# A layer-normalised gated feed-forward block: another form of the normalisation, another split of its first halves, and one late sum on another engine

## The chip, the core and the metric

The kernel runs on one core of a Trainium2 chip. The metric is device time in microseconds (us). Five engines work side by side, each through its own instructions in order: TensorE (PE; its weight loads are listed as PEld), VectorE (DVE), ScalarE (ACT), GpSimd (POOL) and SyncE (SP), which here only issues DMAs.

## What is computed

The input x has 2 x 1024 tokens of 512 features, in fp32. Cut to what matters:

```python
xn  = (x - mean(x)) / sqrt(var(x) + 1e-5)             # per token
s   = einsum('bsk,nk->bsn', xn, weight * block_mask)  # 512 -> 512
nx  = xn * rsqrt(mean(xn**2) + 1e-5) * ln_w
h   = silu(nx @ gate_w.T) * (nx @ up_w.T)             # 512 -> 1792
out = x + s * silu(h @ down_w.T)                      # 1792 -> 512
```

## The kernel before

**Tiles.** The 2048 tokens are four token tiles t of 512, and each of these is four row tiles i of 128 tokens. `xt[t, i]` is a row tile in SBUF: 128 tokens on the partitions, 512 features along the free axis. Token tiles 0 and 1 are normalised in this form and then turned on PE: `transpose` (L173) writes a 128x128 piece into a PSUM bank `pt`, one bank for each block c of 128 features, and `evacuate` (L179) copies the bank to SBUF on ACT. Token tiles 2 and 3 come from memory already transposed and are scaled by rows of factors later; the change leaves their form as it is.

**Products.** The matrix products are done in a seven-product scheme on two levels. An outer product q takes sums of quarters of the operands, and within it an `instance` (L398) does seven inner products m = 1 to 7, in the order 1, 5, 2, 6, 3, 7, 4, into the PSUM banks X, Y and Z. A product is a 128x128 weight against 128x512 moving data; the profile shows each as two records of a matmul. Seven groups g of gate and up weights and an eighth of the masked linear layer make 56 instances: first q = 1 and 2 of every group, then q = 6, 5, 7, 3, 4 of each group. After them seven down instances of 25 to 33 products (L649) and the output follow.

**Who makes the operands.** `inner_b` (L274) makes the sums of the moving data on DVE and POOL; the first of them reads the bank `pt_1_0`, so it needs all four pieces of that bank. `inner_a` (L377) makes the sums of the weights on POOL, `scale_a` (L329) multiplies weights by `ln_w` in two halves of 256 columns (on POOL for group 0, on ACT for the others), and `summed` (L503) adds two partial results of product 7 of each group, for its four quarters i, on the engines that a tuple names.

**The normalisation.** `stats` (L131) makes mean and variance of a row tile on DVE, `stats_act` (L138) does it on ACT for row tile 1 of token tile 0. `factors` (L145) makes, for the four row tiles at once, `scl` = 1/sqrt(var) (a square root on ACT, L161, then a reciprocal on DVE, L158), and `nb` = -mean x scl (on DVE, L159). `normalise` (L163) then writes x x scl + nb over half a row tile, 128x256: L167 on DVE or POOL, L169 on ACT. The eight halves are dealt out by the lists at L782 (token tile 0) and L795 (token tile 1).

**What sets the order.** No scheduler does. Every step is recorded by `at(position, function)`, all steps are sorted by position and emitted in that order (L968), and this is the order on each engine's queue. One position stands for one product of PE; `T` (L748) turns a time in us, counted to 14.0 at position 0, into a position. So a position is an order and not a time: an instruction runs when those before it on its engine and what it waits for are done. Loads go through SP in the order of their positions. One of them, the second group of weights at L763, waits for a small memset on POOL (L761), and the loads of token tiles 2 and 3 stand behind it.

**Warming.** While the first tiles are loaded, PE runs 18 products of the identity (`warm`, L773), as soon as POOL has made the identity (L114).

Of the kernel before, what the change touches and what calls it, by code (L numbers as in the profile page):

```python
# [8 lines left out]
F32 = mybir.dt.float32  # L9
I32 = mybir.dt.int32  # L10
AF = mybir.ActivationFunctionType
ALU = mybir.AluOpType
AX = mybir.AxisListType

P = 128
W = 512
BLK = 32
EPS = 1e-5
# [13 lines left out]
def tile_masked_linear_gated_ffn(  # L32
# [11 lines left out]
    nc = tc.nc  # L44
    NT, H = x.shape
    KC = H // P
    G = gu.shape[0]
    NTT = NT // W
    TT = W // P
# [10 lines left out]
    small = ctx.enter_context(tc.tile_pool(name="small", bufs=2))  # L60
# [8 lines left out]
    def at(pos, fn, *args):  # L69
        events.append((pos, len(events), fn, args))  # L70
# [23 lines left out]
    def bank(tag, name):  # L94
        return ps.tile([P, W], F32, tag=tag, name=name, bufs=PSB[tag])

    def add(eng, o, a, b, op=ALU.add):
        eng.tensor_tensor(o, a, b, op)  # L98

    dve, pool, act = nc.vector, nc.gpsimd, nc.scalar  # L100
# [3 lines left out]
    eps2 = const.tile([P, 1], F32, tag="eps2", name="eps2")  # L104
# [3 lines left out]
    blockones = const.tile([P, P], F32, tag="blockones", name="blockones")  # L108
    keep = const.tile([P, 4, 16], F32, tag="keep", name="keep")

    def constants():
        nc.gpsimd.memset(eps2, EPS * EPS)
        nc.vector.memset(zero, 0.0)
        make_identity(nc, ident)  # L114
        nc.scalar.activation(stat_0, eps2, AF.Sqrt)
        nc.vector.memset(blockones, 0.0)
        for b in range(P // BLK):
            nc.gpsimd.memset(blockones[b * BLK : (b + 1) * BLK, b * BLK : (b + 1) * BLK], 1.0)


    xt, raw, stat = {}, {}, {}
    agg = small.tile([P, NTT, TT, 2], F32, tag="agg", name="agg", bufs=1)
# [22 lines left out]
    def factors(t, i=0, n=TT):  # L145


        if t < 2:
            scl = small.tile([P, n], F32, tag="scl", name=f"scl_{t}_{i}", bufs=3)
            nb = small.tile([P, n], F32, tag="nb", name=f"nb_{t}_{i}", bufs=3)  # L150
        else:
            scl, nb = fac[:, t - 2, 0, :], fac[:, t - 2, 1, :]
        for k in range(n):
            stat[t, i + k] = (scl[:, k : k + 1], nb[:, k : k + 1])
        rows = slice(i, i + n)

        def last():
            nc.vector.reciprocal(scl, scl)  # L158
            nc.vector.scalar_tensor_tensor(nb, agg[:, t, rows, 0], -1.0, scl, ALU.mult, ALU.mult)  # L159

        return [lambda: nc.scalar.activation(scl, agg[:, t, rows, 1], AF.Sqrt, bias=eps2, scale=1.0 + EPS), last]  # L161

    def normalise(t, i, eng, cols=slice(0, W)):  # L163
        scl, nb = stat[t, i]
        v = xt[t, i][:, cols]
        if eng is not act:
            eng.tensor_scalar(v, v, scl, nb, ALU.mult, ALU.add)  # L167
            return
        nc.scalar.activation(v, v, AF.Identity, bias=nb, scale=scl)  # L169

# [292 lines left out]
    def group(g, where):  # L463
        def tiles(i):
            return lambda k: mem[:, i + k, :]

        acc, v5, c1 = tiles(F["acc"] + 4 * (g % 2)), tiles(F["v5"] + 4 * (g % 2)), tiles(F["c1"] if g % 2 else F["vc"])
        vc = tiles(F["tmp"] + 2 if g % 2 else F["vc"])
        h11 = tiles(F["a1"])
        gate = {}  # L470

        def silu(key, t):
            gate[key] = bank("V", f"gate_{g}_{key[2]}")
            nc.scalar.activation(gate[key], t(), AF.Silu)  # L474

        hs, hpos = {}, {}

        def h_out(key, a, b, n):
            nc.vector.tensor_mul(a(), gate[key], b())  # L479
            hs[key] = a()  # L480
            q = {(0, 0): 1, (1, 0): 2, (1, 1): 3}.get(key[:2])
            if q:
                nc.sync.dma_start(h_dram[HD[q], g, n], a())

        def done(R, Hh, tiles):

            ready = {}

            def after(i, pos):
                r, n = divmod(i, 2)  # L490
                if g == G:
                    at(pos + 1, lambda: nc.sync.dma_start(s_dram[2 * R + r, 2 * Hh + n], tiles(i)))
                    return
                ready[i] = pos
                if n in ready and n + 2 in ready:
                    key = (R, Hh, n)
                    p = max(ready[n] + 1.2, ready[n + 2] - 0.5, SILU)
                    at(p, silu, key, lambda: tiles(n))
                    hpos[key] = max(p, ready[n + 2]) + (3.9 if key == (1, 1, 0) else 1.3)
                    at(hpos[key], h_out, key, lambda: tiles(n), lambda: tiles(n + 2), n)  # L500
            return after

        def summed(dst, src, into, then=None, engines=(pool,) * 4):  # L503

            def after(i, pos):
                at(pos + 1.2, lambda: add(engines[i], into(i), dst(i), src(i)))
                if then:
                    then(i, pos + 3.2)
            return after

        nothing = lambda i, pos: None
        setup = {
            1: (None, acc, nothing),
            2: (acc, c1, done(0, 0, c1)),
            6: (acc, acc, nothing),
            5: (None, v5, summed(v5, acc, vc)),
            7: (acc, acc, summed(v5, acc, v5, done(1, 1, v5), (dve, dve, pool, pool) if g < G else (pool,) * 4)),
            3: (vc, vc, done(0, 1, vc)),
            4: (acc, acc, done(1, 0, acc)),
        }  # L520
        for q in setup:
            instance(where[g, q], g, q, *setup[q])

        def h_sum(q, n, tile_of, a, b):

            o = hs[q, n] = tile_of()
            add(pool, o, hs[a + (n,)], hs[b + (n,)], ALU.subtract)
            nc.sync.dma_start(h_dram[HD[q], g, n], o)

        sums, rest = slots(F["acc"] + 4 * (g % 2), 4), 7 * where[g, BLOCKS[0]]  # L530
        at(7 * where[g, 1] + 15, lambda: nc.sync.dma_start(acc_dram[g], sums))
        at(rest - (14 if g else 6), lambda: nc.sync.dma_start(sums, acc_dram[g]))
        if g < G:
            def again():
                nc.sync.dma_start(slots(F["a1"], 2), h_dram[HD[1], g].rearrange("n p w -> p n w"))
                hs.update({(0, 0, n): h11(n) for n in range(2)})
            at(rest + 24, again)
            pos = 0
            for n in (1, 0):
                for q, t, i, a, b in ((5, vc, n + 2, (0, 1), (0, 0)), (7, v5, n + 2, (1, 1), (0, 1)),  # L540
                                      (6, vc, n, (1, 1), (5,))):
                    pos = max(pos, hpos[0, 1, n], hpos[1, 1, n]) + 1.45
                    at(pos, h_sum, q, n, lambda t=t, i=i: t(i), a, b)
            for n in (1, 0):
                pos = max(pos, hpos[1, 0, n]) + 1.45
                at(pos, h_sum, 4, n, lambda n=n: acc(n + 2), (1, 0), (6,))
# [201 lines left out]
    T = lambda us: (us - 14.0) / 0.86  # L748
# [30 lines left out]
    at(T(4.2), stats_act, 0, 1)  # L779
    for t, p, step in ((1, T(11.9), 0), (3, 23.2, 0.6), (2, 36.1, 1.2)):  # L780
        plan(p, step, factors(t))
    for us, i, h, eng in ((7.45, 3, 0, dve), (7.46, 2, 0, dve), (7.45, 0, 0, act), (7.95, 1, 0, act), (8.45, 0, 1, act), (7.47, 1, 1, dve),  # L782
                          (8.5, 2, 1, pool), (8.6, 3, 1, pool)):
        at(T(us), normalise, 0, i, eng, slice(h * W // 2, (h + 1) * W // 2))
    for us, i, cs in ((7.96, 3, (0,)), (7.97, 0, (0,)), (7.98, 2, (0,)), (7.99, 1, (0,)), (8.70, 3, (1,)), (8.71, 0, (1,)), (8.72, 2, (1,)),
                      (8.73, 1, (1,)), (9.25, 0, (2, 3)), (9.26, 1, (2, 3)), (9.7, 2, (2, 3)), (9.71, 3, (2,)), (9.72, 3, (3,))):
        for c in cs:
            at(T(us) + 0.0001 * c, transpose, 0, c, i, "XYYX"[c])
    for i in range(TT):
# [2 lines left out]
        at(T(8.2 + 0.82 * i), stats, 1, i)  # L792
        for c in range(KC):
            at((T(14.35), T(14.8), T(15.25), 4.1)[c] + 0.06 * i, transpose, 1, c, (2, 0, 3, 1)[i], "XVVV"[c])
    for us, i, h, eng in ((12.3, 2, 0, dve), (12.4, 3, 0, dve), (12.5, 2, 1, dve), (12.4, 0, 0, act), (12.5, 1, 0, act),  # L795
                          (12.6, 0, 1, act), (12.6, 3, 1, pool), (12.7, 1, 1, pool)):
        at(T(us), normalise, 1, i, eng, slice(h * W // 2, (h + 1) * W // 2))
    at(T(6.0), scale_a, 0, 0, pool, (0,))
    at(T(8.7), scale_a, 0, 0, pool, (1,))
    at(T(10.3), scale_a, 0, 1, pool)  # L800
    for c in range(KC):
# [20 lines left out]
    for n, p0 in ((1, 31), (0, 50)):  # L822
        t = 2 + n
# [24 lines left out]
    for g in range(G + 1):  # L848
# [8 lines left out]
        if g:  # L857
            plan(p - 7, 1, inner_a(g, 1))
        else:
            for us, fn in zip((10.0, 10.0, 12.5, 12.5), inner_a(0, 1, 0, 1)):  # L860
                at(T(us), fn)
            plan(2.75, 0, inner_a(0, 1, 1, 1))
        ahead = 2 if g == G else 0
# [151 lines left out]
```

## Time and profile before

| what | value |
|---|---|
| three runs | 505.7, 506.1, 506.34 us; median 506.1 us |
| profiled execution | 506.55 us, of which the span of the instructions is 504.7 us |
| PE busy | 498.9 us, 99% |
| DVE / ACT / POOL busy | 379.6 (75%) / 187.6 (37%) / 356.4 (71%) us |
| granted TensorE clock | 1.00 |
| PE records | 784 of the products at L408, mean 593 ns, one started every 0.43 us where nothing holds them |
| DMA | 124.75 MB, 247 GB/s over the span |

The times of a profile count from the first instruction, so the span leaves out 506.55 - 504.7 = 1.85 us around it. PE's matmuls overlap, and a matmul that waits inside this pipeline hardly shows as idle time. So PE is not read by its busy share here but by the starts of its instructions: four 128x512 records in 1.72 us are the steady step, and whatever a piece of the chain takes above this is a wait. A line of the timeline is: start, length, engine, line, operation, output<-inputs, how many in a row; in brackets the engine's idle time before it and what ended it. A line of the chain of waits is: start, length, and what the chain spent it on.

### The profile page before, as it was taken

How to read it: one execution, taken by the hardware profiler on the slowest of the kernel's cores; microseconds unless marked ns; L12 is line 12 of the kernel's file. 1: busy time of each engine (PE TensorE's matmuls, PEld its weight loads, DVE VectorE, ACT ScalarE, POOL GpSimd, SP SyncE). 2: the span in 40 equal slices, each digit the busy share in tenths (PEclk: the TensorE clock that was granted, in tenths of full speed). 3: DMA queues.
4: the chain of work that ended last, by engine and by line, in shares of the span. 5: the costliest groups of instructions: out<-in, count | busy, mean ns of one | idle time of the engine just before them, and what ended most of it. 6: DMA issues, size and time to landing. Idle time of an engine off the chain costs nothing.

```text
span 504.7 us, 4924 instructions
## 1 busy us (share of the span) xinstructions
PE 498.9 (99%) x1223; PEld 226.7 (45%) x1223; DVE 379.6 (75%) x582; ACT 187.6 (37%) x363; POOL 356.4 (71%) x301
## 2 busy tenths in 40 slices
PE   8999999999999999999999999999999999999997
PEld 7444444444444444444444444444444444444444
DVE  6977887876968969697896989969647644377636
ACT  5666776634535363343535342330100101001111
POOL 4728997464896959879696988975672764649960
PEclk9999999999999999999999999999999999999999
DMA  6879847268168595866959594699996798467372
GB/s 213 295 234 339 293 169 249 113 251 304 62 232 308 187 309 194 303 237 234 307 188 311 190 317 161 227 352 369 359 336 230 239 394 309 133 247 265 108 229 86
DMA packets 62365, 124.75 MB, mean 247 GB/s; under 512 B 5984, under 2 KB 13824, under 8 KB 60288
## 3 DMA queue, kind: packets, MB, share of 16 engines
q1 hardware_dynamic: 62192, 124.43, 69.7%
q8 instruction: 10, 0.16, 0.1%
q14 instruction: 19, 0.16, 0.1%
q10 hardware_dynamic: 144, 0.00, 0.0%
HBM read 78.25 MB, written 46.15 MB: 247 GB/s over the span
## 4 chain that ended last, share of the span: by engine, by line
PE 97%; DVE 1%; DMA 1%; SPq 0%; issue 0%; ACT 0%; ACTq 0%
PE x L408 38%; PE y L408 19%; PE dx L656 15%; PE z L408 10%; PE dy L656 8%; PE dz L656 5%; PE dv L656 1%; PE pt L176 1%; DMA mem<-in_x 1%; PE part L667 1%; DVE st L133 0%; DVE mem L167 0%; SPq L129 0%; DVE agg L134 0%; ACT scl L161 0%
## 5 line engine op out<-in xcount | busy, mean ns | idle before, releaser
L98 POOL TENSOR_TENSOR mem<-mem 128x512 f32<-128x512 f32 (+4 forms) x261 | 322.4, 1258 | 111.5 <-ACT mem L436 30.5
L408 PE MATMUL x<-mem 128*128 128x512 f32 x448 | 211.6, 593 | 0.0
L408 PEld LDWEIGHTS x<-mem 128*128 128x128 f32 x448 | 84.4, 190 | 107.2 <-issue 89.9
L98 DVE TENSOR_TENSOR mem<-x,mem 128x512 f32<-128x512 f32 x137 | 93.4, 686 | 39.0 <-PE x L408 37.4
L408 PE MATMUL y<-mem 128*128 128x512 f32 x224 | 114.6, 593 | 0.1
L656 PE MATMUL dx<-mem 128*128 128x512 f32 x174 | 78.3, 592 | 0.0
L98 DVE TENSOR_TENSOR mem<-mem 128x1536 f32<-128x1536 f32 (+3 forms) x51 | 67.0, 1318 | 6.9 <-PE dx L656 4.4
L98 DVE TENSOR_TENSOR mem<-y,mem 128x512 f32<-128x512 f32 x96 | 65.9, 686 | 7.6 <-PE y L408 6.1
L415 ACT COPY z<-x 128x512 f32<-128x512 f32 x54 | 31.0, 573 | 94.7 <-PE x L408 90.7
L408 PEld LDWEIGHTS y<-mem 128*128 128x128 f32 x224 | 42.2, 190 | 53.1 <-issue 46.7
L408 PE MATMUL z<-mem 128*128 128x512 f32 x112 | 57.2, 593 | 0.0
L656 PEld LDWEIGHTS dx<-mem 128*128 128x128 f32 x174 | 33.1, 190 | 41.6 <-issue 41.1
L656 PE MATMUL dy<-mem 128*128 128x512 f32 x98 | 44.5, 592 | 0.0
L474 ACT ACTIVATE gate<-mem 128x512 f32<-128x512 f32 x56 | 32.7, 602 | 20.4 <-DVE mem L98 15.9
L479 DVE TENSOR_TENSOR mem<-gate,mem 128x512 f32<-128x512 f32 x56 | 38.2, 683 | 1.9 <-ACT gate L474 1.5
L629 POOL TENSOR_TENSOR mem<-mem 128x512 f32<-128x512 f32 x16 | 25.5, 1602 | 14.0 <-DMA mem<-s_dram 13.8
L639 ACT ACTIVATE silu<-mem 128x512 f32<-128x512 f32 (+1 forms) x16 | 9.2, 575 | 64.3 <-DVE mem L98 48.0
L408 PEld LDWEIGHTS z<-mem 128*128 128x128 f32 x112 | 21.1, 190 | 25.8 <-issue 21.9
L98 DVE TENSOR_TENSOR mem<-z,mem 128x512 f32<-128x512 f32 x41 | 28.1, 685 | 2.6 <-PE z L408 2.5
L656 PEld LDWEIGHTS dy<-mem 128*128 128x128 f32 x98 | 18.6, 190 | 23.4 <-issue 23.4
L98 DVE TENSOR_TENSOR mem<-dx,mem 128x512 f32<-128x512 f32 x16 | 11.1, 692 | 20.5 <-PE dx L656 20.4
L656 PE MATMUL dz<-mem 128*128 128x512 f32 x56 | 25.2, 592 | 0.0
(94 smaller groups left out, 287.6 us busy)
## 6 DMA issues: line engine op xcount, KB each, us to landing
h_dram<-mem SPq DMA_DIRECT2D x98, 256.0 KB, 2.4
mem<-h_dram SPq DMA_DIRECT2D x28, 768.0 KB, 6.3
mem<-in_gu SPq DMA_DIRECT2D x42, 256.0 KB, 4.1
acc_dram<-mem SPq DMA_DIRECT2D x8, 1024.0 KB, 4.0
mem<-acc_dram SPq DMA_DIRECT2D x8, 1024.0 KB, 6.2
mem<-in_x_t SPq DMA_DIRECT2D x24, 256.0 KB, 5.5
mem<-in_x SPq DMA_DIRECT2D x16, 256.0 KB, 4.6
s_dram<-mem SPq DMA_DIRECT2D x16, 256.0 KB, 5.6
```

Source lines behind the costliest of these rows:

```text
L98: eng.tensor_tensor(o, a, b, op)
L176: nc.tensor.transpose(pt[t, c][:, i * P : (i + 1) * P], xt[t, i][:, c * P : (c + 1) * P], ident)
L408: nc.tensor.matmul(st[key], weights(g, q, m), operand(q, m), start=first and not (key == "z" and seeded), stop=True, skip_group_check=True)
L415: nc.scalar.copy(st["z"], st["x"])
L474: nc.scalar.activation(gate[key], t(), AF.Silu)
L479: nc.vector.tensor_mul(a(), gate[key], b())
L629: at_later.append(lambda: nc.gpsimd.tensor_tensor(s_tile, s_tile, rms_bc[t], ALU.mult))
L639: nc.scalar.activation(b[0][:, part], y[:, part] if source is None else source(), AF.Silu)
L656: nc.tensor.matmul(st[key], w(), b(), start=first and key != "z", stop=True, skip_group_check=True)
L667: nc.tensor.matmul(st[part.start][:, part], w(), b()[:, part], start=False, stop=True, skip_group_check=True)
```

## The change

1. **Form.** `normalise` on DVE and POOL becomes (x - mean) x scl, straight from the statistics and the reciprocal. For token tiles 0 and 1 DVE no longer makes `nb`.
2. **ScalarE's own shift.** ACT still needs scl and a shift. `minus_mean` makes -mean of one row tile ahead of time, and `shift_act` multiplies it by scl: both are ACT instructions of one element per partition. For token tile 0 row tile 0 gets them, for token tile 1 row tiles 0 and 3.
3. **Split of the halves.** Token tile 0: the first half of row tile 1 goes from ACT to POOL, ahead of POOL's first scaling of weights; ACT keeps two halves, POOL has three. Token tile 1: the first half of row tile 1 goes from ACT to POOL and the second half of row tile 3 from POOL to ACT.
4. **Order on PE and POOL.** The third and fourth transposes of row tile 1 of token tile 0 come after the first product instead of before it; nothing else of PE's order changes. On POOL the fourth weight sum of group 0 comes after the normalisation of token tile 1. SP's order of DMAs is the same.
5. **Constants.** The memset of `eps2` and two of the four of `blockones` go from POOL to DVE.
6. **One late sum.** For group 6 (g = G - 1) the sum of quarter i = 1 in `summed` goes from DVE to POOL.

```diff
     def constants():
-        nc.gpsimd.memset(eps2, EPS * EPS)
+        nc.vector.memset(eps2, EPS * EPS)
...
-            nc.gpsimd.memset(blockones[b * BLK : (b + 1) * BLK, b * BLK : (b + 1) * BLK], 1.0)
+            (nc.vector, nc.gpsimd)[b % 2].memset(blockones[b * BLK : (b + 1) * BLK, b * BLK : (b + 1) * BLK], 1.0)
...
         def last():
             nc.vector.reciprocal(scl, scl)
-            nc.vector.scalar_tensor_tensor(nb, agg[:, t, rows, 0], -1.0, scl, ALU.mult, ALU.mult)
+            if t > 1:
+                nc.vector.scalar_tensor_tensor(nb, agg[:, t, rows, 0], -1.0, scl, ALU.mult, ALU.mult)
...
+    minus = small.tile([P, 2, TT], F32, tag="minus", name="minus", bufs=1)
+
+    def minus_mean(t, i):
+        nc.scalar.mul(minus[:, t, i : i + 1], agg[:, t, i, 0:1], -1.0)
+
+    def shift_act(t, i):
+        scl, nb = stat[t, i]
+        nc.scalar.activation(nb, scl, AF.Identity, scale=minus[:, t, i : i + 1])
...
         if eng is not act:
-            eng.tensor_scalar(v, v, scl, nb, ALU.mult, ALU.add)
+            eng.tensor_scalar(v, v, agg[:, t, i, 0:1], scl, ALU.subtract, ALU.mult)
             return
...
-            7: (acc, acc, summed(v5, acc, v5, done(1, 1, v5), (dve, dve, pool, pool) if g < G else (pool,) * 4)),
+            7: (acc, acc, summed(v5, acc, v5, done(1, 1, v5), (dve, dve if g < G - 1 else pool, pool, pool) if g < G else (pool,) * 4)),
...
-    for us, i, h, eng in ((7.45, 3, 0, dve), (7.46, 2, 0, dve), (7.45, 0, 0, act), (7.95, 1, 0, act), (8.45, 0, 1, act), (7.47, 1, 1, dve),
+    at(T(5.0), minus_mean, 0, 0)
+    at(T(7.44), shift_act, 0, 0)
+    for us, i, h, eng in ((7.45, 3, 0, dve), (7.46, 2, 0, dve), (7.45, 0, 0, act), (7.46, 1, 0, pool), (7.95, 0, 1, act), (7.47, 1, 1, dve),
                           (8.5, 2, 1, pool), (8.6, 3, 1, pool)):
...
-                      (8.73, 1, (1,)), (9.25, 0, (2, 3)), (9.26, 1, (2, 3)), (9.7, 2, (2, 3)), (9.71, 3, (2,)), (9.72, 3, (3,))):
+                      (8.73, 1, (1,)), (8.80, 0, (2, 3)), (9.7, 1, (2, 3)), (9.71, 2, (2, 3)), (9.72, 3, (2,)), (9.73, 3, (3,))):
...
-    for us, i, h, eng in ((12.3, 2, 0, dve), (12.4, 3, 0, dve), (12.5, 2, 1, dve), (12.4, 0, 0, act), (12.5, 1, 0, act),
-                          (12.6, 0, 1, act), (12.6, 3, 1, pool), (12.7, 1, 1, pool)):
+    for us, i, h, eng in ((12.3, 2, 0, dve), (12.4, 3, 0, dve), (12.5, 2, 1, dve), (12.4, 0, 0, act), (12.5, 1, 0, pool),
+                          (12.6, 0, 1, act), (12.8, 3, 1, act), (12.7, 1, 1, pool)):
...
-    at(T(6.0), scale_a, 0, 0, pool, (0,))
+    for us, i in ((12.35, 0), (12.7, 3)):
+        at(T(11.85) + 0.04 * i, minus_mean, 1, i)
+        at(T(us), shift_act, 1, i)
+    at(T(7.9), scale_a, 0, 0, pool, (0,))
...
-            for us, fn in zip((10.0, 10.0, 12.5, 12.5), inner_a(0, 1, 0, 1)):
+            for us, fn in zip((10.0, 10.0, 12.45, 12.9), inner_a(0, 1, 0, 1)):
```

## The prediction

> **What bounds the kernel now.** I read the page first, then the chain of waits of the first 22 us, then the timelines of single engines there, then the chain piece by piece to the end.
>
> ```profile
> PE 498.9 (99%) x1223; PEld 226.7 (45%) x1223; DVE 379.6 (75%) x582; ACT 187.6 (37%) x363; POOL 356.4 (71%) x301
> PEclk9999999999999999999999999999999999999999
> ```
>
> PE is busy throughout at full clock, and the change leaves its work as it is. Time can only come from waits in its chain, and the chain shows few. In its first part (start, length, what):
>
> ```profile
> 7.48 0.19 DVE scl L158
> ...
> 7.70 0.17 DVE nb L159
> ...
> 7.89 1.23 DVE mem L167 x2
> ...
> 9.16 1.31 PE pt L176 x10
> 10.47 0.94 PE x L408 x2
> 11.42 0.44 PE pt L176 x4
> ...
> 14.43 1.56 PE pt L176 x12
> 15.99 1.04 PE y L408 x2
> ...
> 20.05 0.08 issue
> 20.13 1.10 PE y L408 x2
> ```
>
> Four transposes take 0.44 us where nothing holds them and two product records 0.86. So until 9.16 the end hangs on the normalisation; the twelve transposes hold 1.56 - 1.32 = 0.24 us of waiting, the products after them 0.18, those at 20.05 0.08 + 0.24 = 0.32. After 22 us I find two more places: 0.08 us at 60 us, and this one, in the chain and in DVE's timeline:
>
> ```profile
> 310.28 1.95 PE x L408 x4
> ```
>
> ```profile
> 309.14 1.31 DVE L98 TENSOR_TENSOR mem<-mem 128x512 f32<-128x512 f32 x1
> 310.38 0.68 DVE L98 TENSOR_TENSOR mem<-x,mem 128x512 f32<-128x512 f32 x1
> ```
>
> Four records take 1.95 instead of 1.72 us: the third waits for a PSUM bank that DVE's instruction at 310.38 reads out, and that one stands behind the sum at 309.14. All that the change can touch is worth some 1.5 us of 505.
>
> **Part 1, token tile 0.** The reciprocal ends at 7.66. Without nb, DVE begins at 7.70 instead of 7.89. How long its halves take depends on POOL beside it: by instruction the six of L167 on DVE take 0.41 to 0.65 us, the four on POOL 0.58 to 0.69. Here POOL was at work when DVE began (0.65 each). In the changed kernel both wait for the reciprocal and DVE is first, as in token tile 1, where POOL began 0.07 us after DVE; those three took 0.41, 0.57, 0.65, and POOL's first 0.69. I take these: DVE's ends move from 8.54, 9.11, 9.68 to 8.11, 8.60, 9.16. The form with subtraction is in no row; the same instruction with the other form is the nearest, for both engines.
>
> ACT's shift is a one-element ACTIVATE (0.19 us, the row of L143), so from 7.70 to 7.89, and its first half stays at 8.54; its second ends at 9.04 instead of 9.53, as only two are left. -mean is made in ACT's idle 1.26 us before 7.15 and costs nothing; without that cover 0.1 us. PE: the transposes of bank c = 0 follow 8.60 (DVE), the bank is full at 9.09 instead of 9.60, ACT copies it by 9.71 instead of 10.22, and the first product starts at 9.81 instead of 10.32: 0.51 earlier.
>
> Then POOL. Before:
>
> ```profile
> 7.84 0.55 POOL L325 TENSOR_SCALAR mem<-mem,lnw_sb,zero 128x256 f32<-128x256 f32 x1 [4.02 <-DMA mem<-in_gu]
> 8.38 1.15 POOL L167 TENSOR_SCALAR mem<-mem,scl,nb 128x256 f32<-128x256 f32 x2
> 9.51 0.58 POOL L325 TENSOR_SCALAR mem<-mem,lnw_sb,zero 128x256 f32<-128x256 f32 x1
> 10.18 0.99 POOL L98 TENSOR_TENSOR mem<-mem 128x128 f32<-128x128 f32 x2
> 11.11 0.10 POOL L761 MEMSET mem<- 128x1 f32 x1
> 11.19 1.10 POOL L325 TENSOR_SCALAR mem<-mem,lnw_sb,zero 128x256 f32<-128x256 f32 x2
> ```
>
> There is no idle time over 0.1 us in this stretch, and the third half goes in front of it: 7.77 to 8.45 (0.69), then all that follows 0.60 later. The first scaling (9.0) and the second (10.7) are still early enough. The third ends at 12.36 instead of 11.76, and the product x of the second instance needs it. PE gets there sooner: first product 9.81 to 10.74, six transposes instead of four, z from 11.40 to 12.26. So x waits for POOL until 12.42 (POOL to PE some 0.06) where it stood at 12.55, and after a wait the second record comes 0.53 instead of 0.43 later (15.91 to 16.44 in this trace). The next z then starts at 13.38 (13.41 before) and the transposes of token tile 1 at 14.24 (14.27). **Of the 0.51 us some 0.03 is left**: a new wait on POOL takes the rest.
>
> The Trainium skill, "SBUF — State Buffer", section "Who interferes with whom", speaks against this part: a tensor_scalar of VectorE in a two-port mode and a GpSimd instruction share a pair of ports under an exclusive lock, and the second blocks until the first has ended. The trace agrees only in part: DVE at 7.89 to 8.54 and POOL at 7.84 to 8.40 did 0.41 + 0.55 = 0.96 us of work in 0.70. By the strict lock each DVE half would hold POOL 0.41 us, 1.23 in place of the 0.11 that I count, and the whole sum would be 0.6 us slower than before. I follow the row.
>
> **Part 2, token tile 1.** DVE's statistics follow its halves without idle time, so they end 0.51 earlier, at 12.36 (the last load was issued at 5.66 and takes a median 4.6 us; it is there). ACT must first copy two banks (until 12.56) and make -mean, so scl comes at 12.86 and the reciprocal at 13.07 instead of 13.41. First halves: DVE 13.52 and 14.00 (14.06, 14.55 before), ACT 13.93 (14.25), and row tile 1, which was ACT's second at 14.74, is POOL's at 14.0. So all four are there before PE comes at 14.24, and the 0.24 us of waiting go. The late ones have room: ACT's third half 15.13, needed at 15.36; POOL's second 14.5, needed at 15.5. Bank c = 0 is full at 14.84 instead of 15.12; DVE's sum from it (0.69) ends at 15.57, and y starts at 15.63 instead of 15.91. From there DVE has no gap over 0.11 us until 22.5, and the wait at 20.05 hangs on it, so it moves with the rest and stays. **Parts 1 and 2: -0.28 us.**
>
> **Hidden.** The memsets on DVE and POOL (0.06 to 0.2 us) stand before 2.1 us; DVE's first load ends its wait at 3.53, and the warming ends 0.6 us before the first transpose. The memset at 11.11 moves to 11.72, and with it 14 loads that SP holds behind it (SP waited 4.6 us there). The weights among them are first used by ACT at 18.89 (issued 11.24, some 4 us to land), row tile 0 of token tile 3 by DVE at 23.69 (landed at 20.5): 3 us of cover; without it up to 0.6 us. POOL's fourth weight sum goes to 14.4, in an idle stretch of 1.83 us.
>
> **Part 3, the late sum.** Without it DVE reads out the bank at some 309.1 instead of 310.38, as PE's product ended at 308.57; the wait of **0.23 us goes**, and what comes behind it on DVE moves up as well. On POOL the sum falls into an idle 1.23 us before 311.13 (1.27 us, the row of POOL's sums), and the one beside it (1.99, where its like take 1.54) runs without DVE's. Its reader on ACT goes from 310.49 to about 311.2; DVE needs that at 314.5.
>
> **The sum.** -0.28 - 0.23 = -0.51: the profiled 506.55 becomes 506.05. The median of the runs is 0.45 lower than that execution: 506.1 - 0.5 = **505.6 us**. Bounds of the one unknown that counts, POOL's half with subtraction (three of them ahead of x): from 0.46 (its 128x128 sum), where x isn't held and y comes at 15.35, in all -0.8; to 1.27 (its 128x512 sum), in all -0.51 + 3 x 0.69 = +1.56. I take 0.58, the same shape and class.
>
> **Rivals.** 0.2% is 1.0 us, about what a measurement can tell from no change.
> - Forecast, 505.6: 0.52.
> - POOL doesn't hold x (its halves or hops shorter by 0.1): 505.3; 0.15. For it: a wait of only 0.16 us. Against: POOL has no gap to make good in.
> - As before, and the wait at 20.05 goes too, which hangs on DVE's row of sums: -0.8 - 0.32, so 505.0; 0.14. Against: seven sums in a row at 0.6 us.
> - One half gives nothing, the head or the late sum (POOL late with its next sum): 505.85; 0.12.
> - Slower: the subtracting form is dear on POOL. Place: the x at 12.42. Price: 3 x (d - 0.58); from d = 0.75 it eats the gain, from 1.08 it is slower by 1.0; at 1.27, 507.7; 0.07. For it: POOL's two-input sums cost twice DVE's (1.27 against 0.68). Against: one tensor input, 0.58.
>
> So faster by over 0.2%: 0.14; within: 0.79; slower: 0.07. The range 505.0 to 506.2 takes in all but the slow case and half of the third, and the 0.3 us by which the runs differ.
>
> **What would show it.** First product at 9.8; x of the second instance held by POOL's L325 at about 12.4; twelve transposes in 1.32 us from 14.2; y at 15.6; 1.72 us for the four records at 310. Wrong, if POOL's halves take over 0.7 us, if a transpose waits for POOL, if DVE waits for a load near 23, or if the step at 310 stays 1.95.

## The result, and the profile after

The changed kernel takes **507.99 us** (median of 7 runs, 507.92 to 508.72) against 506.27 us for the kernel before (median of 7 runs, 505.7 to 506.97). The ratio is 1.0035, interval 1.0024 to 1.0047: it is slower by 1.7 us. The prediction was 505.6 with a range to 506.2; what came is the rival it had given 0.07, the dear subtraction on GpSimd. The profiled execution took 507.99 us with a span of 506.1 us. Line numbers have moved: L177 is `normalise` on DVE and POOL, L179 the same on ACT, L171 the shift, L186 the transposes, L335 POOL's scaling of weights, L418 the products.

Of the page of the changed kernel, first the engines, then the chain that ended last by engine, then the group of the products x (count, busy time and mean ns, idle time before it and what ended it):

```profile
PE 499.1 (99%) x1223; PEld 226.1 (45%) x1223; DVE 378.4 (75%) x582; ACT 188.0 (37%) x368; POOL 361.8 (71%) x300
...
PE 96%; POOL 2%; DMA 1%; issue 0%; DVE 0%; ACT 0%; POOLq 0%
...
L418 PE MATMUL x<-mem 128*128 128x512 f32 x448 | 211.5, 593 | 0.6 <-POOL mem L335 0.5
```

PE's work is what it was; POOL is busy 5.4 us longer and stands for 2% of the chain, and the products x name POOL's scaling as what they waited for. The view of the line of `normalise` (engine, operation, count, shortest/median/longest ns, first and last start):

```profile
L177 DVE TENSOR_SCALAR mem<-mem,agg,scl x6: 400/413/570, 7.3 to 14.4; 128x256 f32<-128x256 f32 x6
L177 POOL TENSOR_SCALAR mem<-mem,agg,scl x5: 1217/1225/1402, 7.4 to 16.4; 128x256 f32<-128x256 f32 x5
```

The answer is in the second line. DVE's halves cost what they cost before (0.41 us where nothing disturbs them); POOL's take 1.22 us, where the four of the kernel before took 0.58 to 0.69, as the same view of that kernel shows:

```profile
L167 POOL TENSOR_SCALAR mem<-mem,scl,nb x4: 582/583/688, 8.4 to 14.4; 128x256 f32<-128x256 f32 x4
```

The chain of waits of the first 24 us of the changed kernel (start, length, what) shows where that goes:

```profile
7.41 1.37 POOL mem L177
8.78 0.54 POOL mem L335
9.32 2.41 POOL mem L177 x2
11.73 0.55 POOL mem L335
...
13.40 0.50 issue
13.90 0.85 POOL mem L335
14.76 0.46 POOL mem L98
15.22 2.42 POOL mem L177 x2
17.64 0.04 issue
17.68 0.33 PE pt L186
18.01 0.86 PE y L418 x2
```

From the reciprocal to y the chain now runs on POOL, which was nowhere in it before. (The profile puts the start of POOL's first half down to a load of weights that landed at 7.34; but this half starts 0.11 us after the reciprocal here and in e2, e6 and e8 below, so I take the reciprocal for what it waited for.) PE waits for POOL five times, and the timeline of PE names it in the brackets (idle time before, and what ended it) at three of them:

```profile
11.79 0.44 PE L186 MATMUL pt<-ident,mem 128*128 128x128 f32 x2 [0.36 <-POOL mem L177]
...
13.99 1.12 PE L418 MATMUL x<-mem 128*128 128x512 f32 x2 [0.54 <-POOL mem L335]
...
16.48 1.53 PE L186 MATMUL pt<-ident,mem 128*128 128x128 f32 x9 [0.18 <-POOL mem L177]
```

The other two are transposes at 8.84, behind POOL's first half that ended at 8.78, and at 17.68. The x of the second instance starts at 13.99 (12.55 before), y at 17.85 (15.91), the y of the second instance at 21.82 (20.13). The wait of 0.245 us before that one has shrunk to 0.09. The four records that stood at 310.28 are at 311.96 now, and in the chain of the changed kernel their stall is gone:

```profile
311.96 1.72 PE x L418 x4
```

So the two profiles differ by +1.68 at the y of the second instance, -0.24 at 310, together +1.44, and that is the difference of their last PE instructions (501.15 and 502.59).

**A clock for comparing profiles.** The first loads do not land at the same time in every execution: the reciprocal of token tile 0 ends between 7.18 and 8.02 us in the nine profiles here (7.66 before, 7.27 after). I therefore count from its end as well. By that the change costs 1.83 us (from 493.49 to 495.32 us until PE's last instruction), which agrees with the 1.72 of the medians. The times in this table are in us; x2 is the first x of the second instance (in the lines of a profile, x2 at the end still means two in a row), y the first y.

| kernel | median (runs) | ratio, interval | reciprocal ends | to first product | to x2 | to y | to PE's end |
|---|---|---|---|---|---|---|---|
| before | 506.27 (7), later 506.19 (27 and 21) | | 7.66 | 2.66 | 4.89 | 8.25 | 493.49 |
| changed | 507.99 (7) | 1.0035, 1.0024 to 1.0047 | 7.27 | 2.62 | 6.71 | 10.58 | 495.32 |
| e2, quick form on POOL | 505.73 (11) | 0.9995, 0.9986 to 1.0004 | 7.18 | 2.34 | 4.81 | 8.19 | 493.02 |
| e3, old form, new split | 506.11 (11) | 1.0000, 0.9991 to 1.0009 | 7.23 | 2.34 | 5.12 | 8.33 | 493.34 |
| e4, late sum alone | 505.98 (11) | 1.0000, 0.9991 to 1.0009 | 7.37 | 2.53 | 4.76 | 7.99 | 493.00 |
| e5, before with subtraction on POOL | 507.23 (11) | 1.0020, 1.0011 to 1.0029 | 7.58 | 2.48 | 4.92 | 9.06 | 493.86 |
| e6, changed without the late sum | 508.46 (5) | 1.0045, 1.0032 to 1.0059 | 7.35 | 2.61 | 6.70 | 10.57 | 495.56 |
| e7, e2 with one half on DVE | 506.15 (11) | 0.9998, 0.9989 to 1.0007 | 8.02 | 2.34 | 4.79 | 7.99 | 493.32 |
| e8, quick form in token tile 1 | 507.99 (5) | 1.0035, 1.0022 to 1.0047 | 7.59 | 2.61 | 6.70 | 9.91 | 494.91 |

### The profile page after: what moved, and what is told of

The parts are those of the page before. It is cut to its first block, busy times and chain, and to the rows that moved or that the text cites. A ratio compares the mean times of both kernels' runs of the same rounds, so it can differ in the third digit from the quotient of the medians.

```text
span 506.1 us, 4930 instructions
## 1 busy us (share of the span) xinstructions
PE 499.1 (99%) x1223; PEld 226.1 (45%) x1223; DVE 378.4 (75%) x582; ACT 188.0 (37%) x368; POOL 361.8 (71%) x300
## 4 chain that ended last, share of the span: by engine, by line
PE 96%; POOL 2%; DMA 1%; issue 0%; DVE 0%; ACT 0%; POOLq 0%
PE x L418 38%; PE y L418 19%; PE dx L666 15%; PE z L418 9%; PE dy L666 8%; PE dz L666 5%; POOL mem L177 1%; PE dv L666 1%; PE part L677 1%; DMA mem<-in_gu 1%; DMA mem<-in_x 1%; POOL mem L335 0%; POOL mem L98 0%; PE pt L186 0%; DVE mem L656 0%
## 5 line engine op out<-in xcount | busy, mean ns | idle before, releaser
L418 PE MATMUL x<-mem 128*128 128x512 f32 x448 | 211.5, 593 | 0.6 <-POOL mem L335 0.5
L418 PEld LDWEIGHTS x<-mem 128*128 128x128 f32 x448 | 84.6, 190 | 107.9 <-issue 90.7
L418 PE MATMUL y<-mem 128*128 128x512 f32 x224 | 114.5, 592 | 0.0
L418 PEld LDWEIGHTS y<-mem 128*128 128x128 f32 x224 | 42.2, 190 | 52.8 <-issue 46.6
L418 PE MATMUL z<-mem 128*128 128x512 f32 x112 | 57.3, 594 | 0.1
L418 PEld LDWEIGHTS z<-mem 128*128 128x128 f32 x112 | 21.1, 190 | 26.2 <-issue 21.2
```

The source lines that it names most:

```text
L418: nc.tensor.matmul(st[key], weights(g, q, m), operand(q, m), start=first and not (key == "z" and seeded), stop=True, skip_group_check=True)
```

## The experiments

The profile left four theories of why POOL's halves took twice as long: the subtraction itself, the mean read as a strided element of `agg`, the order of the two operations, and DVE at work beside POOL. The theory I held was the first.

**e1: the forms by themselves.** A kernel that computes only the statistics of four row tiles and then runs the forms one after the other; all else of the reference is left out.

```python
pool.tensor_scalar(o, h, scl[:, 0:1], nb[:, 0:1], ALU.mult, ALU.add)                # L77
pool.tensor_scalar(o, h, agg[:, 0, 0:1], scl[:, 0:1], ALU.subtract, ALU.mult)       # L79
pool.tensor_scalar(o, h, mean[:, 0:1], scl[:, 0:1], ALU.subtract, ALU.mult)         # L81
pool.tensor_scalar(o, h, minus[:, 0:1], scl[:, 0:1], ALU.add, ALU.mult)             # L83
pool.tensor_scalar(o, h, scl[:, 0:1], ms[:, 0:1], ALU.mult, ALU.subtract)           # L85
pool.tensor_scalar(o, h, agg[:, 0, 0:1], None, ALU.subtract)                        # L87
pool.tensor_scalar(o, h, scl[:, 0:1], None, ALU.mult)                               # L89
```

Expected:

> This kernel leaves out all of the work but the statistics of four row tiles; it then runs GpSimd's tensor_scalar in several forms with VectorE idle, VectorE's forms with GpSimd idle, and both together. Theory A (subtraction is dear on GpSimd): mult-then-add and add-then-mult take 0.58 us for 128x256 as in the profile before, every form with a subtraction about 1.2. Theory B (only mult-then-add is quick): add-then-mult takes 1.2 as well. Theory C (the stride of the mean's operand): subtract-then-mult with the mean copied to a plain row takes 0.58. Theory D (VectorE beside it): all forms take 0.58 alone and 1.2 only where VectorE runs too. At 512 columns a dear form would be near 2.4, if the cost goes by the element.

Measured, in the timeline of POOL in this kernel (start, length, engine, line, operation; DVE is idle from 8.2 to 26.9). Each form runs twice, on two row tiles, so L78 is the form of L77 again, and L91 to L94 are the first two forms over 512 columns:

```profile
8.79 0.56 POOL L78 TENSOR_SCALAR side<-mem,scl,nb 128x256 f32<-128x256 f32 x1
9.33 1.22 POOL L79 TENSOR_SCALAR side<-mem,agg,scl 128x256 f32<-128x256 f32 x1
...
11.73 1.22 POOL L81 TENSOR_SCALAR side<-mem,mean,scl 128x256 f32<-128x256 f32 x1
...
14.13 0.55 POOL L83 TENSOR_SCALAR side<-mem,minus,scl 128x256 f32<-128x256 f32 x1
...
15.20 1.23 POOL L85 TENSOR_SCALAR side<-mem,scl,ms 128x256 f32<-128x256 f32 x1
...
17.61 0.93 POOL L87 TENSOR_SCALAR side<-mem,agg 128x256 f32<-128x256 f32 x1
...
19.41 0.93 POOL L89 TENSOR_SCALAR side<-mem,scl 128x256 f32<-128x256 f32 x1
...
21.98 0.76 POOL L92 TENSOR_SCALAR side<-mem,scl,nb 128x512 f32<-128x512 f32 x1
22.72 2.08 POOL L93 TENSOR_SCALAR side<-mem,agg,scl 128x512 f32<-128x512 f32 x1
```

The subtracting form takes 1.22 with DVE idle and with the mean copied to a dense tile (L81), so neither the neighbour nor the stride makes it. Two operations in the other order, add then multiply, take 0.55 (L83), and multiply then subtract 1.23 (L85), so it isn't the order. Wherever a subtraction stands in the pair, the instruction is dear. At 512 columns it is 2.08 against 0.76, so 256 further columns cost 0.86 against 0.21: the price grows with the data. On DVE both forms take 0.40 to 0.41. One thing doesn't fit "the subtraction alone": a single multiplication takes 0.92 to 0.93 too (L89), as dear as a single subtraction. What the runs show is that the two pairs of multiply and add are quick and the other forms tried are not.

**e2: the quick form of the same arithmetic on GpSimd.** The changed kernel; DVE keeps the subtraction, POOL adds -mean, which ACT makes for three more rows of token tile 0 (of which POOL uses all) and one of token tile 1.

```diff
-        if eng is not act:
+        if eng is pool:
+            eng.tensor_scalar(v, v, minus[:, t, i : i + 1], scl, ALU.add, ALU.mult)
+            return
+        if eng is dve:
             eng.tensor_scalar(v, v, agg[:, t, i, 0:1], scl, ALU.subtract, ALU.mult)
...
+    at(T(5.1), minus_mean, 0, 1)
+    at(T(6.75), minus_mean, 0, 2)
+    at(T(6.76), minus_mean, 0, 3)
+    at(T(11.95), minus_mean, 1, 1)
```

> The changed kernel, but GpSimd's halves are (x + minus mean) times scale, with minus mean from ScalarE, and VectorE keeps the subtraction. Theory A: GpSimd's halves take 0.58 us, the product x of the second instance starts near 12.4 from the same landing of the loads, and the time is 0.4 to 0.6 us below before, about 505.8. Theory B: halves of 1.2 us and a time like the changed kernel's, 508.0.

Measured: 505.73 us, 2.26 less than the changed kernel (the slowest run here, 506.98, lies below the fastest there, 507.92) and 0.46 less than before, though the interval of the ratio to before takes in no change. The timeline of POOL in this kernel:

```profile
7.29 0.69 POOL L177 TENSOR_SCALAR mem<-mem,minus,scl 128x256 f32<-128x256 f32 x1 [3.41 <-DVE scl L158]
7.96 0.58 POOL L338 TENSOR_SCALAR mem<-mem,lnw_sb,zero 128x256 f32<-128x256 f32 x1
8.52 1.12 POOL L177 TENSOR_SCALAR mem<-mem,minus,scl 128x256 f32<-128x256 f32 x2
```

Two halves in 1.12 us here took 2.42 in the changed kernel. From the reciprocal, x2 comes 1.90 us sooner (6.71 to 4.81): three halves at 0.64, 1.92. At y it is 2.39 sooner, at PE's end 2.30. The price of one form of one instruction on one engine is thus the whole of the loss, and more than it. In the chain of this kernel POOL is not to be found. Behind the first product three small waits remain: at x2, which started at 11.99, just behind POOL's third scaling that ended at 11.94 (0.03, and the second record 0.10 later), at the transposes of 15.09 (for ACT's third half, which ended at 15.04) and before the y of 19.43:

```profile
12.13 0.99 PE x L421 x2
...
13.98 1.09 PE pt L189 x10
15.07 0.03 issue
15.09 0.44 PE pt L189 x2
...
19.43 1.10 PE y L421 x2
```

**e3: the old form with the new split.** The changed kernel with x times scl plus nb on all three engines, nb made on DVE again, and without ACT's shift.

```diff
-            if t > 1:
+            if t < 4:
...
-            eng.tensor_scalar(v, v, agg[:, t, i, 0:1], scl, ALU.subtract, ALU.mult)
+            eng.tensor_scalar(v, v, scl, nb, ALU.mult, ALU.add)
```

> The changed kernel with the old form: VectorE makes the shift for all row tiles, all engines multiply and add; the new split of the halves, the new orders and the late sum stay. If the form alone made the loss: GpSimd's halves 0.58 to 0.69, no wait over 0.2 us for them, 0.2 to 0.4 us below before, about 506.0. Rival (the third half on GpSimd in front of the weights makes the loss): at or above before, 506.3 to 508.

Measured: 506.11 us, 0.08 below before, with the late sum's share in it. POOL's halves take 0.56 to 0.86. x2 waits for POOL's scaling here as in the changed kernel, only less long: 12.36 behind a scaling that ended at 12.31. Against e4, which has the same late sum, it is 0.13 worse by the medians, which is within the noise of the runs, and 0.34 from the reciprocal: the split loads POOL up to the edge by itself, and without the new form no gain of it shows.

**e4: the late sum alone.** The kernel before with the one edit of part 6.

```diff
-(dve, dve, pool, pool) if g < G
+(dve, dve if g < G - 1 else pool, pool, pool) if g < G
```

> Before with the late sum on GpSimd alone. Theory: the 0.23 us wait of four records near 310 us goes (1.72 in place of 1.95) and the time is 0.2 us below before, 506.0 to 506.1. Rival: GpSimd is late with what follows and the wait comes back elsewhere, no difference.

Measured: 505.98 us, a median 0.21 lower; but the ratio is 1.0000 (0.9991 to 1.0009), so the runs alone don't tell it from no change. The trace does: the four records near 310 take 1.72 us in its chain. e6, below, is the counter-test.

**e5: the subtraction on POOL in the kernel before**, and nothing else.

```diff
-        if eng is not act:
+        if eng is pool:
+            eng.tensor_scalar(v, v, agg[:, t, i, 0:1], scl, ALU.subtract, ALU.mult)
+            return
+        if eng is dve:
             eng.tensor_scalar(v, v, scl, nb, ALU.mult, ALU.add)
```

> The kernel before, with its own split of the halves and its own late sum; only GpSimd's four halves take the subtracting form. If the form alone is dear: each half 1.22 instead of 0.58, so GpSimd's third scaling, behind two halves, ends at 12.29 + 1.28 = 13.57 and the x of the second instance starts at about 13.6 instead of 12.55; GpSimd's second pair of halves ends at about 16.9, y at about 17.05 instead of 15.91. The wait of 0.245 at the y of the second instance then goes into it. Sum +0.9 to +1.15: 507.2 to 507.4. Rival, that the split (five halves on GpSimd, the third and fifth new) is what costs: within 0.2 of 506.2.

Measured: 507.23 us, +1.04, as expected in size; the rival, that the split costs, falls. In place the expectation missed. It took POOL's fourth scaling, which ended at 12.29 before, for the third, which ended at 11.76; and in the profiled execution the first scaling came before the halves (7.20), not behind the reciprocal. So x2 is hardly late (12.49), and the loss comes at the transposes of token tile 1. The chain of this kernel:

```profile
13.81 2.61 POOL mem L167 x2
16.43 0.04 issue
16.47 0.33 PE pt L179
16.80 0.86 PE y L411 x2
```

Against e4, whose head is that of the kernel before and whose first scaling ran early as well, y is 1.07 us later from the reciprocal (9.06 and 7.99). At PE's end 0.86 of it is left (493.86 and 493.00), and 0.62 without the 0.24 of the late sum: the waits that e4 has at its y and at the y of the second instance, 0.1 and 0.34, are gone here. This execution, 506.76, is one of the faster of e5's (506.52 to 507.76); why the median is higher by more than 0.62, no trace here shows.

**e6: the changed kernel without the late sum.** The tuple of part 6 is put back.

```diff
-(dve, dve if g < G - 1 else pool, pool, pool) if g < G
+(dve, dve, pool, pool) if g < G
```

> The changed kernel with its late sum back on VectorE: the first half of the change alone. If the parts add up: the changed kernel's 507.99 and the 0.21 to 0.24 that the late sum gave alone, 508.2; the stall before the four records at 310 is back. Rival, that the late sum costs beside the slow halves (it is on the engine that is now late): 507.9 or less.

Measured: 508.46 us, 0.47 above the changed kernel by the medians, 0.24 from the reciprocal to PE's end. The rival falls: the late sum still pays beside the slow halves. In the chain of this kernel the four records are long again:

```profile
312.04 1.96 PE x L418 x4
```

**e8: the quick form in token tile 1 alone.** The changed kernel; POOL's three halves of token tile 0 subtract, its two of token tile 1 add.

```diff
-        if eng is not act:
+        if eng is pool and t == 1:
+            eng.tensor_scalar(v, v, minus[:, t, i : i + 1], scl, ALU.add, ALU.mult)
+            return
+        if eng is not act:
...
+    at(T(11.95), minus_mean, 1, 1)
```

> The changed kernel, in which GpSimd's two halves of token tile 1 alone take the quick form (x plus minus mean) times scale; its three halves of token tile 0 still subtract. If most of the loss is made in token tile 0, by the third scaling that comes late behind three slow halves: x of the second instance still at 13.99, transposes of token tile 1 from 15.81 without a wait, y at 15.81 + 12 x 0.109 + 0.15 = about 17.25 instead of 17.85; 507.99 - 0.6 = 507.4, and up to 507.65 if the wait before the y of the second instance (0.245 in the kernel before) comes back with it. Rival, that the halves of token tile 1 make most of the loss: 506.7 or less.

Measured: 507.99 us, the same median as the changed kernel. But the reciprocal came 0.32 later in its profile; from there y is 0.67 sooner than in the changed kernel (9.91 and 10.58) and PE's end 0.41 sooner, the difference being the wait before the y of the second instance, back at 0.245. The chain of this kernel shows the twelve transposes without a wait behind an x that is as late as ever:

```profile
14.29 1.13 PE x L421 x2
15.42 0.86 PE z L421 x2
16.28 1.31 PE pt L189 x12
17.59 1.04 PE y L421 x2
```

So by the profiles most of the loss is made by the three halves of token tile 0 (1.90 us at x2, which this kernel leaves as it was). The 0.35 to 0.6 us that the medians were expected to gain don't show in these five runs, 507.62 to 508.56.

**e7: a better version?** e2 with the second half of row tile 3 of token tile 1 on DVE, which was idle from 13.95 to 14.45, and without ACT's shift for that row.

```diff
-                          (12.6, 0, 1, act), (12.8, 3, 1, act), (12.7, 1, 1, pool)):
+                          (12.6, 0, 1, act), (12.6, 3, 1, dve), (12.7, 1, 1, pool)):
...
-    for us, i in ((12.35, 0), (12.7, 3)):
+    for us, i in ((12.35, 0),):
```

> The adding form on GpSimd (505.73 in its own run) with the second half of row tile 3 of token tile 1 on VectorE instead of ScalarE, whose shift and copy of the mean go with it. VectorE was idle from 13.95 to 14.45 there. If ScalarE's third half is what the transposes waited for at 15.09 (0.19): y at 15.18 instead of 15.37 and the time 505.5. Rival, that the y of the second instance, which waited 0.18 at 19.43, is late for a reason of its own: the gain goes into that wait and the time stays at 505.7.

Measured: 506.15 us, no better than before. The first step is as worked out: y comes at 7.99 from the reciprocal instead of 8.19. But the y of the second instance comes at 12.22 instead of 12.25: its wait has grown and taken the gain, as the rival said. The profile also has a new wait of 0.34 us at 47, where a y follows a small transpose of the factors; the timeline of PE there:

```profile
47.04 0.27 PE L237 MATMUL fac_rows<-ident,fac 128*8 128x128 f32 x1
47.39 1.13 PE L421 MATMUL y<-mem 128*128 128x512 f32 x2
```

Its chain puts that on a sum of DVE that ended at 47.34. In DVE's queue this sum comes behind L160, which multiplies four elements per partition for the factors. L160 took 1.30 us in e7 and 0.37 in e2 (the timelines of DVE, e7 first):

```profile
45.43 1.30 DVE L160 SCALAR_TENSOR_TENSOR fac<-agg,fac 128x4 f32<-128x4 f32 x1
...
44.62 0.37 DVE L160 SCALAR_TENSOR_TENSOR fac<-agg,fac 128x4 f32<-128x4 f32 x1
```

The same instruction on another token tile, at 33 us, takes 0.16 with POOL idle. At 45 us POOL is in the middle of its sums of two tensors, and in all nine profiles this instruction ends 0.02 us after one of them ends: in e7 at 46.74, after a sum of POOL from 45.44 to 46.72 that began 0.01 behind it. Its length goes from 0.18 to 1.30 with the moment at which the two meet, and only in e7 did it reach PE. So the 0.34 is a meeting of two engines in this execution; without it PE's end would be where e2 has it (493.32 - 0.34 = 492.98, e2 493.02). Whether the edit makes such a meeting likelier is not shown.

## Why the prediction was wrong

**The step that failed** is the term for "POOL's half with subtraction": "I take 0.58, the same shape and class". It measured 1.22 alone and 1.40 for the first beside DVE. The bounds were right (0.46 to 1.27), and so was the place, "the x at 12.42": x2 was held by POOL's third scaling. The choice between the bounds was wrong. Shape and class were the same, one tensor and two scalars, 128x256; the pair of operations was not, and no row of the trace before showed that pair on POOL. The argument "against: one tensor input, 0.58" had nothing measured behind it, since both known rows were multiply and add; 0.07 was far too little for a cost that no row showed, with five of these instructions on an engine that had no idle time over 0.1 us where the first three fell. The term is about the whole miss: 507.99 - 505.6 = 2.39, of which the quick form in e2 gives 2.26 back.

**The rival was itself too cheap.** It priced 3 x (1.22 - 0.58) = 1.92, so -0.51 + 1.92 = +1.41. The changed kernel against e2, from the reciprocal: +1.90 at x2, as the rival has it, then 0.49 more at y, -0.09 as the wait before the second y shrinks: +2.30 at PE's end, and 2.26 by the medians. The 0.49 are the two halves of token tile 1, which the rival left out; e8 takes them out alone and y gains 0.67, more by the 0.19 that e2 loses at ACT's third half just before its y.

**Part 1** with quick halves (e2): the first product comes 2.34 us after the reciprocal, forecast 9.81 - 7.66 = 2.15, before 2.66. The term that was off is ACT's shift: 0.29 us, not the 0.19 of the row of L143, so ACT's first half ends at 8.20 and the transposes behind it start 1.07 after the reciprocal where 0.94 was worked out: 0.13 of the 0.19 that was missed. The Trainium skill, "ScalarE: Activation LUTs", section "What ACT_TABLE_LOAD costs", says that each operand given as a column of per-partition values adds about 93 ns to a fixed 186; the shift takes such a scale and needs 279 to 296 ns here, -mean takes none and needs 186 to 216, so the runs agree. x2 comes 4.81 after the reciprocal, forecast 4.76. "A new wait on POOL takes the rest" was right in kind: x2 starts 0.05 after POOL's third scaling. Its size was 0.03 where 0.16 was forecast, as the late first product had used up the rest; that x2 comes so near the forecast is two errors cancelling.

**Part 2** (e2): "So all four are there before PE comes at 14.24" holds, ten transposes run without a wait; the late half that had "room" did not have it. ACT's second shift is 0.28 as well, its third half ends at 15.04 and the last two transposes wait 0.19 for it. The forecast of -0.28 for parts 1 and 2 stands beside -0.25 between the medians of e2 and e4; but from the reciprocal the two profiles end alike (493.02 and 493.00). Part of what the profile before showed as waits hung on weights that landed late in that one execution: POOL's first scaling was at 7.84 there, after the reciprocal, and at 7.06 in e4, before it. So whether the head gains a quarter of a microsecond or nothing stays open, and that e2's 505.73 lies near the forecast of 505.6 doesn't prove these two parts.

**Part 3**: forecast -0.23. By the traces it was right: the four records take 1.72 us with the late sum on POOL and 1.95 or 1.96 without, and the changed kernel ends 0.24 before e6 from the reciprocal. The runs of e4 alone (a median 0.21 lower, ratio 1.0000) are too noisy to show it.

**Hidden**: right. The memset at 11.11 moved to 13.28, further than the 11.72 I worked out, and SP's loads behind it to 13.42, 2.2 us later than before; PE shows no wait over 0.05 us from y at 17.85 to 62 us but the 0.09 at 21.82.

**The lock.** The prediction followed the row, not the strict rule of the Trainium skill, "SBUF — State Buffer", section "Who interferes with whom". For this instruction e1 bears that out: with both engines at work DVE's 0.41 and POOL's 0.55 together repeat every 0.565 us, a little more than POOL's alone, and not their sum. (Whether DVE's instruction ran in a two-port mode, which the rule asks for, no trace shows.) That one engine waits for the other to the end does occur on this chip, as L160 in e7 shows, but between other instructions. The loss has nothing to do with it, as L79 of e1 shows with DVE idle.

## What to carry to other kernels

The cost of an instruction on GpSimd goes with its pair of operations, not only with its shape: measure the exact form before giving it five times to an engine that has no idle time, and if it is dear, write the same arithmetic as multiply and add. A cost that no row shows should not be set to the kindest neighbour; when one end of its bounds turns the sign, that end deserves a chance to match. And count the unknown in every place where it occurs: here the places behind the first wait added another half microsecond.

## What the runs showed of the hardware

- GpSimd, `tensor_scalar` on 128x256 fp32: 0.55 us for multiply-add and add-multiply; 1.22 for subtract-multiply and multiply-subtract; 0.92 for a multiplication or a subtraction alone, so one operation is dearer than the quick pair. At 128x512: 0.76 and 2.08 for the first two.
- VectorE takes 0.40 to 0.41 us for either form, one started every 0.32.
- Beside each other, in multiply-add `tensor_scalar`, both engines start an instruction every 0.565 us, DVE's lengthened to 0.64, POOL's to 0.58.
- A VectorE product of four elements per partition from two SBUF tensors (`scalar_tensor_tensor`, L159 or L160) takes 0.16 us with GpSimd idle. Beside GpSimd's sums of two tensors it took 0.18 to 1.30 us in nine profiles and ended 0.02 us after one of these sums each time.
- The end of the first loads moves by up to 0.8 us between executions (reciprocal at 7.18 to 8.02), more than most of the terms in the sum: differences of a quarter of a microsecond are better read from a common event in the trace than from single spans.
